# Strassen products in four PSUM banks: the second product moves from the first bank into the free half of the fourth

## The chip, the cores and the metric

The kernel runs on one core of one Trainium2 chip. The metric is device time in microseconds (us), the median of several executions; lower is better. The engines are named as in the profile: PE is TensorE (matrix products), PEld its weight loads, DVE is VectorE, ACT is ScalarE, POOL is GpSimd, SP is SyncE, which issues most of the transfers.

PSUM is the memory that TensorE writes its results to. [...] Here each accumulator is one bank, and it is used as two halves of 256 columns.

## The reference

Four graph layers run one after the other on 4096 nodes with 256 features, each as `x = layernorm(x + layer(x))`. Cut to the layers that the change touches, numbered from 0:

```python
# layer 2: one additive head
h = x @ W
e = leaky_relu((h @ a[:D])[:, None] + (h @ a[D:])[None, :], 0.01)
attention = softmax(where(adj > 0, e, -1e12), axis=1)
x = layernorm(x + elu(attention @ h))

# layer 3: cosine attention
att = softmax(where(adj > 0, cos(x @ Wk.T, x @ Wq.T), -9e15), axis=1)
x = layernorm(x + 0.5 * (att @ x) + 0.5 * x)      # every row of adj has a one
```

In both the heavy part is a product of a 4096 x 4096 matrix of weights with the 4096 x 256 features.

## The kernel before

The program is one function that works through the four layers. Layers 2 (`additive_one`) and 3 (`cosine_attention`) share the code that the change edits.

**Tiling.** The 4096 target nodes are cut into 8 blocks of 512 (index `b`). The 4096 source nodes are cut into 32 tiles of 128, taken in pairs: 16 steps `g` per block. For a pair of source tiles the weights are a tile `z` of 128 x 2 x 512 (`prob`), unnormalised; the features are two tiles of 128 x 256. What is summed over the 16 steps is the transposed output of the block, 256 features by 512 targets.

**Strassen's form.** A step is a 2 x 2 product: two source tiles, two halves of the features, two halves of the targets. Done plainly it takes eight products of 128 x 128 by 128 x 256. The kernel uses a Strassen form with seven. For this, `mix_weights` makes four combinations `s` of the weights in each step, and `mix_features` makes four combinations `t` of the features once per layer. `product` (line 440) issues product number `n` of seven; a table gives the accumulator `at`, the half, the stationary operand `w` and the moving operand `a`. An fp32 product appears in the trace as two matmul records. In layer 2, block 0 is done plainly and blocks 1 to 7 in Strassen's form; in layer 3 all eight blocks are, except for the last two steps of the last block.

**Banks before.** There are four accumulators `acc0` to `acc3`, one bank each, with one buffer each. Product 1 goes to the first half of `acc3`, products 2 and 3 to the two halves of `acc0`, products 4 and 5 to `acc1`, 6 and 7 to `acc2`. (The code counts them 0 to 6.) The second half of `acc3` is unused. The `start` flag, given with the first product that goes to a bank in step 0, begins a new sum.

**Taking the result out.** After step 15 the output quarters `c[:, 0]` to `c[:, 3]` are made by ScalarE and VectorE. `first_half` (line 449) copies product 1 out of `acc3` with ScalarE (`one`, line 451), adds it to both halves of `acc0` with one VectorE addition of 512 elements (line 452), and then adds the two halves of `acc1` one after the other (lines 454 and 455). `second_half` (line 457) adds the first half of `acc2` to two quarters (459) and its second half to one (460). As each accumulator has one buffer, the first product of the next block that writes a bank has to wait until the reads of that bank are done.

**Order of the work.** In layer 2 the order of instructions on TensorE, VectorE and ScalarE is as written out in the program (`manual_schedule`, line 649). `sums` (572) runs three steps behind `weights` (549), which makes the weights: ScalarE line 566, VectorE line 567, and the combinations with VectorE line 436 and POOL lines 437 and 438. At a block's last step `sums` comes ahead of the new block's `weights`. In layer 3 a planner in the compiler orders each engine's instructions for all but the ending; `outputs` (1184) takes a block's result out and sends its quarters through transposes (line 1151, in `squares_far`) to memory and back. `ending` (1191) does the last block, in written order again: there TensorE adds the quarters to sums that it has begun directly (line 1208). At the change from layer 2 to layer 3, the last block's quarters are projected (line 596) and finished (lines 602 to 614), while the first scores of layer 3 (line 1118) and its feature combinations (lines 429 to 432) are made.

Of the kernel before, what the change touches and what calls it, by code (L numbers as in the profile page):

```python
# [9 lines left out]
FP = mybir.dt.float32  # L10
# [4 lines left out]
OP = mybir.AluOpType  # L15
# [3 lines left out]
P = 128  # L19
# [9 lines left out]
def kernel(  # L29
# [27 lines left out]
    nc = tc.nc  # L57
# [4 lines left out]
    def pool(stack, name, bufs, **kw):  # L62
        return stack.enter_context(tc.tile_pool(name=name, bufs=bufs, reuse_waits="tile", **kw))
# [115 lines left out]
    def begin_root(mv):  # L179
        n = mv.shape[1]  # L180
        v = fin.tile([P, n], FP, name=f"v{n}")
        nc.vector.tensor_scalar_add(v, mv[:, :, 1], EPS)
        return v, first_root(v, n), n
# [240 lines left out]
    HW = QW // 2  # L424
# [15 lines left out]
    def product(acc, z, s, t, g, n):  # L440

        even, odd = X[:, 2 * g, :D], X[:, 2 * g + 1, :D]
        at, half, w, a = ((3, 0, even[:, :P], z[:, 0, :HW]), (0, 0, odd[:, :P], z[:, 1, :HW]),
                          (0, 1, t[:, 1], s[:, 2]), (1, 0, t[:, 0], s[:, 1]), (1, 1, odd[:, P:], s[:, 3]),
                          (2, 0, t[:, 2], s[:, 0]), (2, 1, t[:, 3], z[:, 1, HW:]))[n]
        nc.tensor.matmul(acc[at][:, half * HW:(half + 1) * HW], w, a, start=(g == 0 and half == 0),  # L446
                         stop=(g == NP - 1), skip_group_check=True)

    def first_half(c, one, acc):

        nc.scalar.copy(one, acc[3][:, :HW])
        nc.vector.tensor_tensor(c[:, :2, :], one.unsqueeze(1).to_broadcast([P, 2, HW]),  # L452
                                acc[0].rearrange("p (h i) -> p h i", h=2), OP.add)
        nc.vector.tensor_tensor(c[:, 2, :], c[:, 1, :], acc[1][:, :HW], OP.add)
        nc.vector.tensor_tensor(c[:, 3, :], c[:, 2, :], acc[1][:, HW:], OP.add)

    def second_half(c, acc):

        nc.vector.tensor_tensor(c[:, 1:3, :], c[:, 1:3, :], acc[2][:, :HW].unsqueeze(1).to_broadcast([P, 2, HW]), OP.add)
        nc.vector.tensor_tensor(c[:, 1, :], c[:, 1, :], acc[2][:, HW:], OP.add)  # L460

    def quarters(c, k):

        lo = k % 2 * P
        return [c[:, q, lo:lo + P] for q in ((0, 3), (1, 2))[k // 2]]
# [61 lines left out]
    def additive_one(w_sb, ga, tail, op, follow):  # L527

        with ExitStack() as lay:
# [14 lines left out]
            mixed, acc, prob, mix, mvs, roots, kept, drawn, ys, far_y = {}, {}, {}, {}, {}, {}, {}, {}, {}, {}  # L544
# [27 lines left out]
            def sums(b, g):  # L572
                if g == 0:
                    acc[b] = [pa.tile([P, QW], FP, name=f"acc{n}") for n in range(4)]
                if b:
                    for n in range(7):
                        product(acc[b], prob[b, g], mix[b, g], mixed[g // 2][:, g % 2], g, n)
                else:
                    for j in range(2 * g, 2 * g + 2):
                        for c in range(KC):  # L580
                            nc.tensor.matmul(acc[b][c], X[:, j, c * P:(c + 1) * P], prob[b, g][:, j % 2, :],
                                             start=(j == 0), stop=(j == NT - 1))
                if g == NP - 1:
                    c = kept[b] = op.tile([P, 4, HW], FP, name="quarters")
                    if b:
                        first_half(c, op.tile([P, HW], FP, name="one"), acc[b])
                        second_half(c, acc[b])
                    else:
                        nc.scalar.copy(c[:, :2, :], acc[b][0].rearrange("p (h i) -> p h i", h=2))
                        nc.vector.tensor_copy(c[:, 3, :], acc[b][1][:, :HW])  # L590
                        nc.vector.tensor_copy(c[:, 2, :], acc[b][1][:, HW:])
# [57 lines left out]
            with tc.manual_schedule(engines=fixed):  # L649
                for i in range(len(units) + LAG):  # L650
                    b, g = units[i - LAG] if i >= LAG else (-1, 0)
# [440 lines left out]
    def cosine_attention(co, tail):  # L1092
# [4 lines left out]
        with ExitStack() as lay:  # L1097
# [3 lines left out]
            cp = pool(lay, "co_parts", 1)  # L1101
# [7 lines left out]
            mixed, acc, prob, mix, y, back = {}, {}, {}, {}, {}, {}  # L1109
# [73 lines left out]

            def outputs(b):
                c = cp.tile([P, 4, HW], FP, name="quarters")
                first_half(c, cp.tile([P, HW], FP, name="one"), acc[b])
                squares_far(b, 0, (c[:, 0, :], c[:, 3, :]))
                second_half(c, acc[b])
                squares_far(b, 1, (c[:, 1, :], c[:, 2, :]))

            def ending(b):


                c = cp.tile([P, 4, HW], FP, name="quarters")
                pos = [pl.tile([P, QW], FP, name=name)[:, :D] for pl, name in ((ps, "g"), (ps, "g"), (pz, "p"), (pz, "p"))]
                rden = fin.tile([P, QB], FP, name="rden4")
                mv = [fin.tile([P, 2, 2], FP, name=f"mv_end{h}") for h in range(2)]

                def direct(k):
                    for g in range(NP - LAST, NP):  # L1200
                        for n in range(2):
                            nc.tensor.matmul(pos[k], prob[b, g][:, n, k * P:(k + 1) * P],  # L1202
                                             X[:, 2 * g + n, :D], start=(g == NP - LAST and n == 0),
                                             stop=False, skip_group_check=True)

                def others(k):
                    for n, quarter in enumerate(quarters(c, k)):
                        nc.tensor.matmul(pos[k][:, n * P:(n + 1) * P], quarter, ident, start=False, stop=True,
                                         skip_group_check=True)

                def twice_sum(k):
                    junk = cp.tile([P, D], FP, name="one")
                    nc.scalar.activation(junk, pos[k], AF.Copy, scale=2.0 / D, accum_out=rden[:, k:k + 1])

                def row(k):
                    nc.vector.reciprocal(rden[:, k:k + 1], rden[:, k:k + 1])
                    rest(b, k, pos[k], rden[:, k:k + 1], mv[k // 2][:, k % 2, :])

                def roots(h, lo, n):

                    v, r, _ = begin_root(mv[h][:, lo:lo + n])
                    return v, r, n, mv[h][:, lo:lo + n, 0]

                def lifts(v, r, n, mean):
                    end_root(v, r, n, nc.gpsimd)
                    nc.gpsimd.tensor_tensor(v, mean, r, OP.mult)
                    nc.gpsimd.tensor_scalar(v, v, -1.0, 0.0, OP.mult, OP.add)

                def scaled(k, v, r, n):
                    nc.scalar.activation(y[b][:, k, :], y[b][:, k, :], AF.Identity, bias=v[:, n:n + 1], scale=r[:, n:n + 1])  # L1230

                for k in range(2):
                    direct(k)
                first_half(c, cp.tile([P, HW], FP, name="one"), acc[b])
                second_half(c, acc[b])
                for k in range(2):
                    others(k)
                    twice_sum(k)
                    row(k)
                for k in range(2, 4):  # L1240
                    direct(k)
                    others(k)
                twice_sum(2)
                both = roots(0, 0, 2)
                row(2)
                lifts(*both)
                twice_sum(3)
                third = roots(1, 0, 1)
                scaled(0, *both[:2], 0)
                scaled(1, *both[:2], 1)  # L1250
                store(b, 0, 2, nc.sync)
                lifts(*third)
                row(3)
                v, r, _ = begin_root(mv[1][:, 1:])
                scaled(2, *third[:2], 0)
                store(b, 2, 1, nc.sync)
                s = fin.tile([P, 1], FP, name="s_end")
                nc.vector.scalar_tensor_tensor(s, r, v, r, OP.mult, OP.mult)
                nc.vector.tensor_scalar(s, s, -0.5, 1.5, OP.mult, OP.add)
                nc.vector.tensor_tensor(r, r, s, OP.mult)  # L1260
                scale_row(y[b][:, 3, :], mv[1][:, 1:], r, 0)
                store(b, 3, 1, nc.sync)
# [4 lines left out]
            for i in range(len(units) + LAG):  # L1267
                if i < len(units):
                    b, j = units[i]
# [7 lines left out]
                    if (b, j) in steps:  # L1277
                        n, step = steps[b, j]
                        co.prepare(bank, n, step, X[:, n * QB:(n + 1) * QB, :])
                if i >= LAG:  # L1280
                    b, j = units[i - LAG]
# [41 lines left out]
    with ExitStack() as weights1, ExitStack() as den1, ExitStack() as weights3:  # L1323
# [25 lines left out]
        op = weights3.enter_context(tc.tile_pool(name="gb_o", bufs=1))  # L1349
# [37 lines left out]
```

## Time and profile before

| what | value |
|---|---|
| median of 3 runs | 2798.02 us (2794.73 to 2802.38) |
| profiled execution, its own time | 2795.6 us |
| its span, from first to last instruction | 2793.8 us |
| TensorE clock granted | 1.0 |
| layer 2, blocks 1 to 7, in the span | from about 1772 us to 2165 us |
| layer 3, in the span | from about 2165 us to the end |
| copy of product 1 (line 451), ScalarE, 128 x 256 | x15, median 368 ns |
| addition of line 452, VectorE, 128 x 512 | x15, median 687 ns |
| additions of lines 454, 455, 460, VectorE, 128 x 256 | x15 each, medians 422, 417 and 419 ns |
| addition of line 459, VectorE, 128 x 512 | x15, median 681 ns |
| VectorE addition of two SBUF operands, 128 x 256 (line 437, layer 3) | x126, median 424 ns |

All times in the trace are counted from the start of the span. A line such as "1995.72 0.70 PE L446 MATMUL ... x2 [0.94 <-DVE quarters L452]" says: at 1995.72 us, for 0.70 us, TensorE ran two matmul records of line 446; before them it was idle for 0.94 us, and what released it was the VectorE instruction of line 452 that writes `quarters`. The ends of matmuls are modelled, so distances are better read from start to start. Line numbers in the quoted profile are those of the kernel before.

### The profile page before, as it was taken

How to read it: one execution, taken by the hardware profiler on the slowest of the kernel's cores; microseconds unless marked ns; L12 is line 12 of the kernel's file. 1: busy time of each engine (PE TensorE's matmuls, PEld its weight loads, DVE VectorE, ACT ScalarE, POOL GpSimd, SP SyncE). 2: the span in 40 equal slices, each digit the busy share in tenths (PEclk: the TensorE clock that was granted, in tenths of full speed). 3: DMA queues.
4: the chain of work that ended last, by engine and by line, in shares of the span. 5: the costliest groups of instructions: out<-in, count | busy, mean ns of one | idle time of the engine just before them, and what ended most of it. 6: DMA issues, size and time to landing. Idle time of an engine off the chain costs nothing. (4 is left out here: it accounts for less than half of the span.)

```text
span 2793.8 us, 50176 instructions
## 1 busy us (share of the span) xinstructions
PE 2774.1 (99%) x19445; PEld 1427.4 (51%) x19445; DVE 2289.0 (82%) x3040; ACT 1700.7 (61%) x2650; POOL 1052.5 (38%) x986
## 2 busy tenths in 40 slices
PE   9999999999999999999999999999999999999999
PEld 5333333333453333333333333788888777777776
DVE  8899999999677788887888878888887877767676
ACT  7899999999336666666666666465556422222222
POOL 0000100100029878778788793345455000000000
PEclk9999999999999999999999999999999999999999
DMA  7566676665339899998988988567778545445442
GB/s 206 107 142 137 139 144 130 137 143 114 70 97 191 186 178 196 191 188 182 197 182 189 192 181 187 168 198 207 183 207 232 121 76 82 74 71 82 75 72 44
DMA packets 275065, 411.92 MB, mean 147 GB/s; under 512 B 54809, under 2 KB 155657, under 8 KB 273930
## 3 DMA queue, kind: packets, MB, share of 16 engines
q0 software_dynamic: 104176, 182.74, 41.3%
q1 hardware_dynamic: 164280, 218.88, 26.7%
q10 hardware_dynamic: 6370, 7.10, 0.7%
q8 instruction: 152, 2.49, 0.4%
q14 instruction: 87, 0.71, 0.1%
HBM read 335.94 MB, written 39.40 MB: 134 GB/s over the span
## 5 line engine op out<-in xcount | busy, mean ns | idle before, releaser
L834 DVE TENSOR_TENSOR prob<-p,mask 128x1024 f32<-128x1024 f32 x512 | 620.0, 1222 | 166.9 <-ACT p L824 159.9
L824 ACT ACTIVATE p<-p,shift 128x1024 f32<-128x1024 f32 x512 | 557.0, 1090 | 317.8 <-PE p L822 317.1
L312 PE MATMUL acc<-prob,V 128*32 128x512 f32 x6144 | 664.0, 592 | 1.2 <-DVE prob L302 1.2
L299 ACT ACTIVATE prob<-row,dst 128x512 f32<-128x512 f32 x1020 | 635.9, 716 | 0.4
L302 DVE SCALAR_TENSOR_TENSOR prob<-prob,mask 128x2048 f32<-128x2048 f32 x256 | 580.6, 2288 | 25.8 <-ACT prob L299 24.8
L844 POOL TENSOR_TENSOR den<-den,prob 128x1024 f32<-128x1024 f32 x220 | 559.8, 2544 | 92.6 <-DVE prob L834 87.2
L822 PE MATMUL p<-qT,kT 64*64 64x512 f32 x4096 | 531.1, 590 | 2.0 <-DVE prob L834 2.0
L858 PE MATMUL acc<-prob,V 64*64 64x512 f32 x4096 | 529.9, 589 | 0.0
L312 PEld LDWEIGHTS acc<-prob,V 128*32 128x32 f32 x6144 | 197.3, 110 | 453.0 <-issue 432.2
L446 PE MATMUL acc<-mix,mixed 128*128 128x256 f32 x1428 | 388.0, 380 | 2.7 <-DVE quarters L460 1.2
L858 PEld LDWEIGHTS acc<-prob,V 64*64 64x64 f32 x4096 | 157.4, 133 | 282.1 <-issue 280.3
L822 PEld LDWEIGHTS p<-qT,kT 64*64 64x64 f32 x4096 | 154.3, 133 | 278.9 <-issue 256.5
L446 PEld LDWEIGHTS acc<-mix,mixed 128*128 128x128 f32 x1428 | 269.5, 190 | 45.0 <-PE acc L446 3.5
L90 POOL COPY tick<-prob 128x1 f32<-128x1 f32 x35 | 38.0, 1086 | 643.0 <-DVE prob L302 642.1
L1130 DVE TENSOR_TENSOR prob<-prob,mask 128x1024 f32<-128x1024 f32 x128 | 156.2, 1220 | 140.5 <-ACT prob L1122 140.1
L850 POOL DMA_DIRECT2D den<-prob x240 | 232.0, 967 | 61.0 <-DVE prob L834 22.3
L446 PE MATMUL acc<-prob,X 128*128 128x256 f32 x952 | 245.7, 380 | 3.4 <-DVE quarters L452 3.3
L1050 POOL DMA_DIRECT2D mask<-in_adjT x64 | 47.7, 745 | 530.1 <-DVE prob L1130 437.6
L446 PEld LDWEIGHTS acc<-prob,X 128*128 128x128 f32 x952 | 180.1, 190 | 84.1 <-issue 56.7
L567 DVE SCALAR_TENSOR_TENSOR prob<-r,own,mask 128x512 f32<-128x512 f32 x252 | 177.1, 744 | 51.3 <-POOL s L169 13.7
L1122 ACT ACTIVATE prob<-p 128x512 f32<-128x512 f32 x144 | 86.1, 598 | 204.1 <-PE p L1118 202.6
L1122 ACT ACTIVATE prob<-g 128x512 f32<-128x512 f32 x112 | 67.0, 598 | 208.7 <-PE g L1118 208.7
(233 smaller groups left out, 2823.1 us busy)
## 6 DMA issues: line engine op xcount, KB each, us to landing
mask<-in_adjT SPq DMA_DIRECT2D x254, 512.0 KB
den<-prob POOLq DMA_DIRECT2D x240, 512.0 KB, 5.3
mask<-edges SPq DMA_DIRECT2D x512, 64.0 KB
mask<-in_adjT POOLq DMA_DIRECT2D x64, 512.0 KB, 5.7
edges<-in_adj POOLq DMA_DIRECT2D x32, 512.0 KB, 9.6
far<-squares SPq DMA_DIRECT2D x16, 512.0 KB
den<-prob SPq DMA_DIRECT2D x16, 512.0 KB
row<-far SPq DMA_DIRECT2D x7, 1024.0 KB
```

Source lines behind the costliest of these rows:

```text
L299: nc.scalar.activation(z[:, h, :], r, AF.Relu, bias=-1.0, scale=dst[:, j, h:h + 1])
L302: nc.vector.scalar_tensor_tensor(z, z, 1.0, mask[m][:, j % MJ, :].unsqueeze(1).to_broadcast([P, H, QW]), OP.add, OP.mult)
L312: nc.tensor.matmul(acc[b][h * G:(h + 1) * G, n, :], part, prob[b, j][:, h, :], start=(j == 0), stop=(j == NT - 1))
L446: nc.tensor.matmul(acc[at][:, half * HW:(half + 1) * HW], w, a, start=(g == 0 and half == 0), stop=(g == NP - 1), skip_group_check=True)
L567: nc.vector.scalar_tensor_tensor(z[:, n, :], r, ga.own[:, j:j + 1], mask[:, n, :], OP.add, OP.mult)
L822: nc.tensor.matmul(p[c * d:(c + 1) * d, r, :], kT[half, c, at:at + d], qT[half, c, cols], start=True, stop=True)
L824: nc.scalar.activation(p, p, AF.Exp, bias=shift)
L834: nc.vector.tensor_tensor(z, p, mask[m][:, j % MJ, :].unsqueeze(1).to_broadcast([P, KC, QW]), OP.mult)
L844: nc.gpsimd.tensor_tensor(to, to, flat, OP.add)
L850: nc.gpsimd.dma_start(to, flat, accum_op=OP.add)
L858: nc.tensor.matmul(acc[b][c][r * d:(r + 1) * d, :], V[half, j, r * d:(r + 1) * d], prob[b, j][half, r, :], start=(j == 0), stop=(j == NH - 1))
L1130: nc.vector.tensor_tensor(z, z, co.mask[b, 2 * g // MJ][:, lo:lo + 2, :], OP.mult)
```

## The change

Product 2 goes to the second half of `acc3` in place of the first half of `acc0`. `acc0` then holds product 3 alone, in its second half. The start flag is given by product number (n = 0, 2, 3 and 5 begin a bank), which is again the first product of each bank.

`first_half` copies both halves of `acc3` with ScalarE: product 1 to `one`, product 2 straight to quarter 0. VectorE's first addition now makes quarter 1 alone, 256 elements. Quarter 0 still lacks product 1; an addition of 256 elements in SBUF brings it in later: at the end of `second_half` in layer 2 and in the ending, and in `outputs` of layer 3 between `first_half` and the first transposes. This adds, at each of the 15 places where a block is taken out, one ScalarE copy and one VectorE addition, and halves one VectorE addition.

```diff
         even, odd = X[:, 2 * g, :D], X[:, 2 * g + 1, :D]
-        at, half, w, a = ((3, 0, even[:, :P], z[:, 0, :HW]), (0, 0, odd[:, :P], z[:, 1, :HW]),
+        at, half, w, a = ((3, 0, even[:, :P], z[:, 0, :HW]), (3, 1, odd[:, :P], z[:, 1, :HW]),
                           (0, 1, t[:, 1], s[:, 2]), (1, 0, t[:, 0], s[:, 1]), (1, 1, odd[:, P:], s[:, 3]),
                           (2, 0, t[:, 2], s[:, 0]), (2, 1, t[:, 3], z[:, 1, HW:]))[n]
-        nc.tensor.matmul(acc[at][:, half * HW:(half + 1) * HW], w, a, start=(g == 0 and half == 0),
+        nc.tensor.matmul(acc[at][:, half * HW:(half + 1) * HW], w, a, start=(g == 0 and n in (0, 2, 3, 5)),
                          stop=(g == NP - 1), skip_group_check=True)
 
     def first_half(c, one, acc):
 
         nc.scalar.copy(one, acc[3][:, :HW])
-        nc.vector.tensor_tensor(c[:, :2, :], one.unsqueeze(1).to_broadcast([P, 2, HW]),
-                                acc[0].rearrange("p (h i) -> p h i", h=2), OP.add)
+        nc.scalar.copy(c[:, 0, :], acc[3][:, HW:])
+        nc.vector.tensor_tensor(c[:, 1, :], one, acc[0][:, HW:], OP.add)
         nc.vector.tensor_tensor(c[:, 2, :], c[:, 1, :], acc[1][:, :HW], OP.add)
         nc.vector.tensor_tensor(c[:, 3, :], c[:, 2, :], acc[1][:, HW:], OP.add)
 
-    def second_half(c, acc):
+    def second_half(c, acc, one=None):
 
         nc.vector.tensor_tensor(c[:, 1:3, :], c[:, 1:3, :], acc[2][:, :HW].unsqueeze(1).to_broadcast([P, 2, HW]), OP.add)
         nc.vector.tensor_tensor(c[:, 1, :], c[:, 1, :], acc[2][:, HW:], OP.add)
+        if one is not None:
+            nc.vector.tensor_tensor(c[:, 0, :], c[:, 0, :], one, OP.add)
...
                     if b:
-                        first_half(c, op.tile([P, HW], FP, name="one"), acc[b])
-                        second_half(c, acc[b])
+                        one = op.tile([P, HW], FP, name="one")
+                        first_half(c, one, acc[b])
+                        second_half(c, acc[b], one)
...
             def outputs(b):
                 c = cp.tile([P, 4, HW], FP, name="quarters")
-                first_half(c, cp.tile([P, HW], FP, name="one"), acc[b])
+                one = cp.tile([P, HW], FP, name="one")
+                first_half(c, one, acc[b])
+                nc.vector.tensor_tensor(c[:, 0, :], c[:, 0, :], one, OP.add)
                 squares_far(b, 0, (c[:, 0, :], c[:, 3, :]))
                 second_half(c, acc[b])
                 squares_far(b, 1, (c[:, 1, :], c[:, 2, :]))
...
                 for k in range(2):
                     direct(k)
-                first_half(c, cp.tile([P, HW], FP, name="one"), acc[b])
-                second_half(c, acc[b])
+                one = cp.tile([P, HW], FP, name="one")
+                first_half(c, one, acc[b])
+                second_half(c, acc[b], one)
```

## Prediction

> **What bounds the kernel now.** I read the page's busy times first, then the matmul groups of the changed line, then the timeline of one place where an accumulator changes hands. Two shares and the two largest groups of the products' line, from the page:
>
> ```profile
> PE 2774.1 (99%) x19445; PEld 1427.4 (51%) x19445; DVE 2289.0 (82%) x3040; ACT 1700.7 (61%) x2650; POOL 1052.5 (38%) x986
> ...
> L446 PE MATMUL acc<-mix,mixed 128*128 128x256 f32 x1428 | 388.0, 380 | 2.7 <-DVE quarters L460 1.2
> ...
> L446 PE MATMUL acc<-prob,X 128*128 128x256 f32 x952 | 245.7, 380 | 3.4 <-DVE quarters L452 3.3
> ```
>
> TensorE has work in 99% of the span, and all idle time before the products is 6.1 us, most of it released by the output additions of lines 452 and 460. So only time in which TensorE stands still can be won, and the additions are where it stands. The waits view of TensorE says the same: 3.3 us on line 452 (4 waits), 1.2 us on line 460 (6 waits).
>
> The timeline of the handover from block 4 to block 5 in layer 2 (start, duration, engine, line; idle before and its releaser in brackets), TensorE, then VectorE, then ScalarE:
>
> ```profile
> 1993.76 0.59 PE L446 MATMUL acc<-prob,mixed 128*128 128x256 f32 x2
> 1994.19 0.59 PE L446 MATMUL acc<-prob,X 128*128 128x256 f32 x2
> 1995.72 0.70 PE L446 MATMUL acc<-prob,X 128*128 128x256 f32 x2 [0.94 <-DVE quarters L452]
> 1996.26 1.14 PE L446 MATMUL acc<-mix,mixed 128*128 128x256 f32 x4
> 1997.24 0.59 PE L446 MATMUL acc<-mix,X 128*128 128x256 f32 x2
> 1998.04 0.67 PE L446 MATMUL acc<-mix,mixed 128*128 128x256 f32 x2 [0.21 <-DVE quarters L460]
> ```
> ```profile
> 1994.39 0.70 DVE L129 STREAM_TRANSPOSE squares<-rows 128x512 f32<-128x512 f32 x1
> 1995.02 0.65 DVE L452 TENSOR_TENSOR quarters<-one,acc 128x512 f32<-128x512 f32 x1
> 1995.77 0.42 DVE L454 TENSOR_TENSOR quarters<-quarters,acc 128x256 f32<-128x256 f32 x1
> 1996.23 0.42 DVE L455 TENSOR_TENSOR quarters<-quarters,acc 128x256 f32<-128x256 f32 x1
> 1996.75 0.69 DVE L459 TENSOR_TENSOR quarters<-quarters,acc 128x512 f32<-128x512 f32 x1
> 1997.47 0.42 DVE L460 TENSOR_TENSOR quarters<-quarters,acc 128x256 f32<-128x256 f32 x1
> ```
> ```profile
> 1993.63 0.38 ACT L451 COPY one<-acc 128x256 f32<-128x256 f32 x1
> 1993.88 1.52 ACT L566 ACTIVATE r<-other_row,less,dst 128x512 f32<-128x512 f32 x2
> ...
> 1998.59 1.49 ACT L566 ACTIVATE r<-other_row,less,dst 128x512 f32<-128x512 f32 x2 [2.17 <-DVE prob L567]
> ```
>
> A product is two matmul records 0.43 us together; seven make a step of 3.02 us. The first step of a new block is longer. Measured on the timeline from the first product to that of the next step: 3.57, 3.94, 4.75, 4.79, 4.36 and 4.91 us in blocks 2 to 7 of layer 2, which take over from blocks 1 to 6; together 26.3 against 6 x 3.02 = 18.1, so 8.2 us lost. Layer 3's seven handovers take 4.84 us where a usual step takes 4.74, another 0.7 us. In all 8.9 us, 0.32% of the span: the ceiling of this change.
>
> In the shown handover the second product waits for line 452 (bank 0), the fourth starts just after line 455 (bank 1; 1996.70 after 1996.65), the sixth after line 460 (bank 2; 1998.04 after 1997.89). VectorE goes through its five additions without a pause, so their chain, not TensorE, sets when the sixth product starts.
>
> [...]
>
> **The change part by part.**
>
> *Products.* Order, count and sizes stay: seven products of 0.43 us, three of the neighbouring pairs in one bank before and after. Cost 0. The program order on TensorE is the same but for one score matmul pair at the start of layer 3.
>
> *VectorE's first addition, 512 to 256 elements.* In the shown handover 452 to 454 is 0.75 us from start to start; 454 to 455, the 256 form, 0.46. So 0.29 us less, and all that follows on VectorE, through line 460, is 0.29 us earlier.
>
> *The added addition of 256 (c0 + one).* 0.42 us, some 0.34 of it new time in the queue (460 to 567 is 0.34 apart). In layer 2 it stands behind line 460, so no bank waits for it; line 567 behind it is about 0.05 us later (+0.34 - 0.29). What hides it: probabilities are made three steps ahead, and VectorE's steady share is 337 of 393 us there. Without that cover: 6 x 0.05 = 0.3 us.
>
> *ScalarE's second copy.* 0.25 to 0.37 us, and the first product of the new block now waits for both copies. In the shown handover: copies end at about 1994.02 + 0.30, first product 1994.47 instead of 1994.19, third product (the first to need bank 0) free to start at 1995.33. The 256 addition ends at 1995.02 + 0.39 = 1995.41. So ScalarE's delay is hidden, by a tenth of a microsecond only; a copy longer by that would start to show. Behind the copies on ScalarE stand line 566's activations, whose reader is line 567; ScalarE is idle 2.17 us soon after, so 0.37 us is covered. The first copy's later start costs nothing in layer 2, where ScalarE comes to it after the second product has ended.
>
> *Where the stall goes.* Second product: no wait any more. Third: starts 1995.46. Fourth: waits for line 455, now ending 1996.36, so starts 1996.41: a new stall of about 0.4 us that was hidden behind the old one. Sixth: line 460 ends 1997.60, so 1997.75 instead of 1998.04. Of the 1.1 us stall that goes, 0.8 comes back at banks 1 and 2; net 0.29. In the first handover (the 3.57 one) only the fourth and sixth waited; the sixth goes from 1827.79 to 1827.50, again 0.29. Six handovers: 6 x 0.29 = 1.7 us.
>
> *Layer 3.* Here is the VectorE order around a handover:
>
> ```profile
> 2252.89 0.69 DVE L452 TENSOR_TENSOR quarters<-one,acc 128x512 f32<-128x512 f32 x1
> 2253.61 0.45 DVE L1151 STREAM_TRANSPOSE kept<-quarters 128x256 f32<-128x256 f32 x1
> 2254.54 0.42 DVE L454 TENSOR_TENSOR quarters<-quarters,acc 128x256 f32<-128x256 f32 x1 [0.48 <-PE acc L446]
> ```
>
> The new addition stands between the first two: the transpose ends at about 2252.89 + 0.46 + 0.46 + 0.45 = 2254.26, still before 2254.54, when TensorE lets line 454 go. The 0.48 us of idle hides it, and line 460, at whose end the sixth product starts, keeps its time. The first copy starts 0.43 us later (2252.44) and ends 2252.81, before 2252.89; the second ends about 2253.15. ScalarE then waits 1.72 us for the next scores. Cost 0; without the cover, 7 x 0.2 = 1.4 us.
>
> *Layer 2 to 3.* VectorE is full from 2164.5 on and carries the extra addition with no gain (line 454 waits for TensorE there): 0.35 us later. Projections that wait for a freed bank may feel it, 0 to 0.45 us. Against it, a score pair of 0.86 us moves ahead of the projection at 2176.24, which had stalled 0.33 us. I take -0.1. *The end:* the additions end at 2780.51, their reader starts at 2781.68; the extra 0.34 is hidden.
>
> *Sum.* -1.7 - 0.1 = -1.8 us. The profiled execution took 2795.6 us with a span of 2793.8; it would take 2793.8. It lies 2.4 us below the median of the runs, 2798.0, to which I carry the difference: 2796.2.
>
> **Rivals.**
>
> (a) *The gain is taken back.* VectorE starts its chain when its own backlog lets it. If the second copy and the extra addition put that start 0.15 us later in each block, and the fourth product's new stall costs a restart of 0.11 us (the second record after a stall starts 0.32 us after the first, not 0.215), 0.29 shrinks to 0.03: 6 x 0.03 = 0.2 us, so 2797.8, or 2798.2 with a slip of 0.45 us in place of my -0.1 where layer 3 begins. Speaks for it: five of the six handovers wait behind VectorE's one queue. Against: VectorE was idle and waiting for others between blocks (line 567 for POOL, in the waits view of this stage, 37.7 us), so 0.05 us is made good there.
>
> (b) *All handover stalls vanish*: if VectorE's chain came earlier in its queue than I place it, so that banks 1 and 2 are free in time: 2798.0 - 8.9 = 2789.1. Against: line 129 stands before the first addition unchanged, and line 460 follows it by a fixed 2.5 us.
>
> (c) *Slower: ScalarE becomes late.* The first copy waits for one more product (0.43 us) and the second adds 0.37. If ScalarE had nothing to spare, each of 14 handovers would move by 0.80: +11.2, so 2809.2. It decides once ScalarE's idle time behind the copies falls under 0.8 us; the trace shows 2.17 (layer 2) and 1.72 (layer 3), and the first product already waits for line 451 in the handover at 2107.54.
>
> **How the numbers follow.** Forecast 0.55 and (a) 0.26, both within 0.3% (8.4 us, about what a measurement of this kernel can tell from no change); (b) 0.09, just beyond it; (c) 0.10, beyond it. So faster 0.09, same 0.81, slower 0.10. Effect bounds of forecast and (a): -3 (if in four handovers the whole second-product wait of 0.7 were won) to +1, so 2795 to 2799; the three runs spread over 7.7 us, half of it each way about a middle, so 2791 to 2802. (b) and (c) are mostly left out.
>
> **What would show it.** Right: no wait for line 452 before the second product; a wait of the fourth product on line 455 of 0.2 to 0.5 us; first steps near 3.3, 3.65, 4.45, 4.5, 4.1, 4.6 us; layer 3 steps still 4.84. Wrong: waits of TensorE on ScalarE's copies over 0.3 us, or steps lengthened away from the handovers.

## The result, and the profile after

The changed kernel takes 2791.9 us against 2796.1 us for the kernel before, medians of 22 runs each; the three runs of the kernel before in the table ahead, with 2798.0 as their median, are among them. The two medians lie 4.2 us apart. The ratio of the times, which is used from here on, is 0.9987, with a 95% interval of 0.9981 to 0.9993: 3.6 us less (2.0 to 5.3). The profiled execution took 2791.86 us, with a span of 2790.1.

In this section line numbers are those of the changed kernel. The first copy is line 451, the new copy 452, the first addition 453, the added addition 462 (1191 in layer 3); lines 454, 455, 459 and 460 are the same additions as before. Further down the page, 566 and 567 became 568 and 569, 504 became 506, 641 became 644, and 1151 became 1154.

The page of the changed kernel, engine shares and the two groups of products:

```profile
PE 2772.4 (99%) x19445; PEld 1427.4 (51%) x19445; DVE 2286.1 (82%) x3055; ACT 1702.6 (61%) x2665; POOL 1051.2 (38%) x986
...
L446 PE MATMUL acc<-mix,mixed 128*128 128x256 f32 x1428 | 388.6, 380 | 4.3 <-DVE mix L437 1.3
...
L446 PE MATMUL acc<-prob,X 128*128 128x256 f32 x952 | 244.3, 379 | 0.0
```

The idle time before the products that read `prob` is gone (3.4 us before). And VectorE does 15 more instructions, yet is busy 2.9 us less. Halving 15 additions and adding 15 should have cost it time: an estimate from the medians in the table ahead is 15 x (0.424 - 0.265) = 2.4 us more, with 0.265 for 0.687 - 0.422. This is the first sign that something else became shorter.

The waits view of TensorE from 1760 us on (us in total, times, longest):

```profile
PE acc L446 <- DVE mix L437: 1.3, 1, 1.3
PE acc L446 <- DVE quarters L460: 1.2, 6, 0.2
PE acc L446 <- DVE quarters L594: 1.1, 1, 1.1
PE acc L446 <- DVE quarters L455: 0.7, 3, 0.2
```

The 3.3 us on the first addition have become 0.7 us on line 455, in three handovers. The single wait of 1.3 us is in layer 3, where the kernel before had 0.4; the last section comes back to it.

The handover into block 5 again: TensorE, VectorE, ScalarE.

```profile
1991.44 1.03 PE L446 MATMUL acc<-prob,X 128*128 128x256 f32 x4
1992.36 0.67 PE L446 MATMUL acc<-mix,mixed 128*128 128x256 f32 x2
1993.25 0.70 PE L446 MATMUL acc<-mix,mixed 128*128 128x256 f32 x2 [0.22 <-DVE quarters L455]
1993.79 0.59 PE L446 MATMUL acc<-mix,X 128*128 128x256 f32 x2
1994.59 0.67 PE L446 MATMUL acc<-mix,mixed 128*128 128x256 f32 x2 [0.21 <-DVE quarters L460]
```
```profile
1991.83 0.38 DVE L453 TENSOR_TENSOR quarters<-one,acc 128x256 f32<-128x256 f32 x1
1992.32 0.42 DVE L454 TENSOR_TENSOR quarters<-quarters,acc 128x256 f32<-128x256 f32 x1
1992.78 0.42 DVE L455 TENSOR_TENSOR quarters<-quarters,acc 128x256 f32<-128x256 f32 x1
...
1994.03 0.42 DVE L460 TENSOR_TENSOR quarters<-quarters,acc 128x256 f32<-128x256 f32 x1
1994.37 0.42 DVE L462 TENSOR_TENSOR quarters<-quarters,one 128x256 f32<-128x256 f32 x1
```
```profile
1990.43 0.39 ACT L451 COPY one<-acc 128x256 f32<-128x256 f32 x1
1990.68 0.41 ACT L452 COPY quarters<-acc 128x256 f32<-128x256 f32 x1
...
1993.51 0.34 ACTq L644 DMA_DIRECT2D far_y<-y  x1
1995.48 0.78 ACT L568 ACTIVATE r<-other_row,less,dst 128x512 f32<-128x512 f32 x1 [2.00 <-DVE prob L569]
```

Products 1 and 2 run without a gap (one group of four records). Product 4 starts 0.89 us after product 3 instead of 0.43, behind line 455. Product 6 waits for line 460. From the start of the first addition to product 6 it is 2.76 us (1994.59 - 1991.83); before, it was 3.02. All this is as forecast, in this handover. What was not forecast: VectorE began its first addition 0.39 us after product 1 (1991.83 - 1991.44); before, 0.83 us after it.

Layer 3, VectorE around a handover:

```profile
2248.23 0.42 DVE L453 TENSOR_TENSOR quarters<-one,acc 128x256 f32<-128x256 f32 x1
2248.57 0.42 DVE L1191 TENSOR_TENSOR quarters<-quarters,one 128x256 f32<-128x256 f32 x1
2249.02 0.45 DVE L1154 STREAM_TRANSPOSE kept<-quarters 128x256 f32<-128x256 f32 x1
2249.88 0.42 DVE L454 TENSOR_TENSOR quarters<-quarters,acc 128x256 f32<-128x256 f32 x1 [0.41 <-PE acc L446]
```

Line 454 still waits 0.41 us for TensorE, so the added addition is covered. Layer 3's seven handover steps sum to 33.86 us in both traces.

| | before | after |
|---|---|---|
| first steps, blocks 2 to 7 of layer 2 (us) | 3.57 3.94 4.75 4.79 4.36 4.91 | 3.48 3.60 3.61 4.09 4.05 4.05 |
| their sum | 26.3 | 22.9 |
| first product of block 1 (layer 2) to first product of layer 3 | 399.25 | 395.96 |
| start of the span to block 1 of layer 2 | 1772.0 | 1770.9 |

The gain lies in layer 2, 3.3 us of it. The 1.1 us ahead of it falls in code that the change doesn't touch; over the traces of this page, in which that code is the same, the start of block 1 lies anywhere between 1769.9 and 1773.5 us. Layer 3 took 0.75 us longer in the trace after, which has the wait of 1.3 us there.

### The profile page after: what moved, and what is told of

Same layout as the page of the kernel before. It is cut to its first block, busy times and chain, and to the rows that moved or that the text cites. A ratio compares the mean times of both kernels' runs of the same rounds, so it can differ in the third digit from the quotient of the medians.

```text
span 2790.1 us, 50215 instructions
## 1 busy us (share of the span) xinstructions
PE 2772.4 (99%) x19445; PEld 1427.4 (51%) x19445; DVE 2286.1 (82%) x3055; ACT 1702.6 (61%) x2665; POOL 1051.2 (38%) x986
## 3 DMA queue, kind: packets, MB, share of 16 engines
q1 hardware_dynamic: 164280, 218.88, 26.3%
```

## Where VectorE's time went

The same stretch of VectorE's written order, in the handover from block 3 to 4: from the first addition to the second instruction `h<-X,a_row` (line 504 before, 506 after; it reads two operands from SBUF, as line 436 does). Before:

```profile
1937.98 0.65 DVE L452 TENSOR_TENSOR quarters<-one,acc 128x512 f32<-128x512 f32 x1
...
1944.86 1.05 DVE L504 CUSTOM_DVE_ANT_0 h<-X,a_row 128x256 f32<-128x256 f32 x1
...
1947.28 0.85 DVE L436 TENSOR_TENSOR mix<-prob 128x512 f32<-128x512 f32 x1
1948.05 1.72 DVE L504 CUSTOM_DVE_ANT_0 h<-X,a_row 128x256 f32<-128x256 f32 x1
```

and GpSimd beside it:

```profile
1939.06 0.59 POOL L133 DMA_DIRECT2D far<-squares  x1
1943.75 1.12 POOL L137 DMA_DIRECT2D T<-far  x2 [4.10 <-DMA far<-squares]
1944.88 0.74 POOL L437 TENSOR_TENSOR mix<-prob,mix 128x256 f32<-128x256 f32 x1
...
1948.06 0.74 POOL L438 TENSOR_TENSOR mix<-prob,mix 128x256 f32<-128x256 f32 x1
1948.75 0.73 POOL L437 TENSOR_TENSOR mix<-prob,mix 128x256 f32<-128x256 f32 x1
```

After, VectorE and GpSimd:

```profile
1935.49 0.38 DVE L453 TENSOR_TENSOR quarters<-one,acc 128x256 f32<-128x256 f32 x1
...
1941.84 1.70 DVE L436 TENSOR_TENSOR mix<-prob 128x512 f32<-128x512 f32 x1
1943.46 0.41 DVE L506 CUSTOM_DVE_ANT_0 h<-X,a_row 128x256 f32<-128x256 f32 x1
...
1945.23 1.03 DVE L436 TENSOR_TENSOR mix<-prob 128x512 f32<-128x512 f32 x1
1946.19 0.41 DVE L506 CUSTOM_DVE_ANT_0 h<-X,a_row 128x256 f32<-128x256 f32 x1
```
```profile
1936.56 0.59 POOL L133 DMA_DIRECT2D far<-squares  x1
1939.85 1.12 POOL L137 DMA_DIRECT2D T<-far  x2 [2.70 <-DMA far<-squares]
1940.98 0.74 POOL L437 TENSOR_TENSOR mix<-prob,mix 128x256 f32<-128x256 f32 x1
...
1943.68 0.78 POOL L437 TENSOR_TENSOR mix<-prob,mix 128x256 f32<-128x256 f32 x1 [0.70 <-DVE mix L436]
```

GpSimd stores the turned squares to memory (line 133) and loads them back (137). The load waits in GpSimd's own queue until the store has landed: 4.10 us before, 2.70 after. Its combinations (437, 438) stand behind that wait. Before, they came out late and back to back, on top of VectorE's instructions: line 504 took 1.05 and 1.72 us where it takes 0.41 alone. After, the backlog is shorter: over their durations alone (0.69 for line 436, 0.41 for the other) these instructions lose 1.01 and 0.34 us, both on line 436. Before, the two of line 504 lost 0.64 and 1.31, and one of line 436 lost 0.16. That is 1.35 us in place of 2.11.

Not every VectorE instruction is stretched in this way. Line 454, one of whose inputs is an accumulator in PSUM, took its usual 0.42 us beside line 438 of GpSimd, 0.39 us of it at the same time in this handover before (at 1938.73) and all of it after (at 1935.97). Lines 504 and 436, which read both inputs from SBUF, are the stretched ones here. The 1.72 us are the 0.41 of line 504 and 1.31 more, nearly twice the 0.73 of a combination; what holds the instruction up in that time is not shown.

Why did the store land earlier? ScalarE's store of the outputs, `far_y<-y`, stands on its queue behind the copies. Before, it was issued at 1939.41, 0.35 us after GpSimd's store was begun. After, the second copy puts it at 1937.17, 0.61 us after.

```profile
1939.41 0.34 ACTq L641 DMA_DIRECT2D far_y<-y  x1
```
```profile
1937.17 0.34 ACTq L644 DMA_DIRECT2D far_y<-y  x1
```

The DMA view for the stretch from 1.0 to 2.5 us after the issue of the squares' store (packets, MB, share of 16 engines; q0 carries GpSimd's transfers, q10 ScalarE's), before and then after:

```profile
q0 software_dynamic: 79, 0.32, 53.8%
q10 hardware_dynamic: 54, 0.22, 36.6%
```
```profile
q0 software_dynamic: 134, 0.52, 87.3%
q10 hardware_dynamic: 6, 0.02, 4.3%
```

Before, the two stores of 512 KB shared the engines nearly from the start. After, the squares' store went first and had nearly all of them. So a quarter of a microsecond on ScalarE decided whether it landed 4.1 to 4.8 us after its issue or 3.0 (blocks 3 to 7). By the packet times in the traces, the output store's data began to move 1.0 to 1.1 us after its issue before, and 1.8 to 1.9 us after it in the changed kernel, just when the last packet of the squares' store had begun. Why it then waited for the whole of the other store is not shown.

The theory, then: the gain is the order of two stores; it reaches TensorE through GpSimd's wait and VectorE's stretched instructions. The rivals: the bank and the shorter addition (the forecast's reason), or layer 3.

## The experiments

Times are medians. Each ratio is to runs of the kernel before on the same chip beside the experiment's own, which had medians of 2796.7 to 2798.2 us.

**The second copy alone, in the kernel before.** Banks and additions stay; in layer 2, ScalarE copies product 1 once more, to quarter 0, which the first addition then overwrites.

```diff
         nc.scalar.copy(one, acc[3][:, :HW])
+        if spare is not None:
+            nc.scalar.copy(spare, acc[3][:, :HW])
...
-                        first_half(c, op.tile([P, HW], FP, name="one"), acc[b])
+                        first_half(c, op.tile([P, HW], FP, name="one"), acc[b], c[:, 0, :])
```

> The kernel before with one more ScalarE copy of 128 x 256 behind line 451 in layer 2 alone (it writes quarter 0, which the addition of line 452 then overwrites; the result is the same). Products, banks and additions are those of before. Theory (transfer order): the copy puts ScalarE's store of the finished rows (far_y) 0.25 us later, so POOL's store of the turned squares lands about 4.1 us after the first addition instead of 5.2 to 5.9, POOL's combinations collide less with VectorE's operations of two SBUF operands, and VectorE reaches the next handover earlier: first steps of blocks 2 to 7 together about 24.6 us instead of 26.3, time about 1.7 us less. Rival (TensorE's own earlier start is what moves VectorE): landing and steps stay as before, 26.3 to 26.6 us, time 0 to +0.3 us.

Measured: 2792.4 us, ratio 0.9987 (0.9981 to 0.9994), the whole gain without the change. The first steps sum to 21.7 us. The theory had the direction right and the size small: it forecast 24.6 us, and 1.7 us off the time, which is the edge of the 3.6 measured (1.7 to 5.3). The output store is issued 1.68 us after the first addition, as in the changed kernel (1.43 before), and GpSimd's wait in the same block falls:

```profile
1935.22 0.59 POOL L133 DMA_DIRECT2D far<-squares  x1
1938.46 1.12 POOL L137 DMA_DIRECT2D T<-far  x2 [2.65 <-DMA far<-squares]
```

**The change without its second copy.** Banks and additions as changed; quarter 0 is made of twice product 1, so product 2 is left out of it.

```diff
-        nc.scalar.copy(c[:, 0, :], acc[3][:, HW:])
...
-            nc.vector.tensor_tensor(c[:, 0, :], c[:, 0, :], one, OP.add)
+            nc.vector.tensor_tensor(c[:, 0, :], one, one, OP.add)
```

> The changed kernel without the second ScalarE copy (quarter 0 is made of twice product 1 and lacks product 2; that part of the computation is left out), all additions kept. Theory (transfer order): the squares' store lands again 5.2 to 5.9 us after the first addition, and only the shorter first addition is left of the gain: first steps about 24.6 us, time 1.7 us less than before. Rival: the gain is all in the freed bank and the shorter addition, so the steps stay at 22.9 us and the time 3.5 us less than before.

Measured: 2797.0 us, ratio 1.0002 (0.9994 to 1.0011). The gain is gone, though banks and the addition of 256 are there; the 1.7 us that the theory still left to the shorter addition are not seen either (the interval runs from 1.7 us less to 3.1 more). The traced execution took 2805.2 us, 8 more than the median, so the lengths of its blocks say little. The wait of GpSimd is back:

```profile
1941.03 0.59 POOL L133 DMA_DIRECT2D far<-squares  x1
1945.84 1.12 POOL L137 DMA_DIRECT2D T<-far  x2 [4.22 <-DMA far<-squares]
```

In one block of this trace the output store happened to be issued 0.94 us behind GpSimd's, elsewhere 0.32 to 0.34; in that block, the third of the four in the table further down, VectorE's stretch C is 11.1 us, in the others 11.7 to 12.2.

**The change with an addition of 512 again.** The first addition makes quarters 1 and 2 (line 454 then overwrites the latter), which undoes only its halving.

```diff
-        nc.vector.tensor_tensor(c[:, 1, :], one, acc[0][:, HW:], OP.add)
+        nc.vector.tensor_tensor(c[:, 1:3, :], one.unsqueeze(1).to_broadcast([P, 2, HW]),
+                                acc[0][:, HW:].unsqueeze(1).to_broadcast([P, 2, HW]), OP.add)
```

> The changed kernel with its first addition widened to 512 elements again (quarters 1 and 2 both get the sum, quarter 2 is overwritten by the next addition; the result is the same). By the prediction's term of 0.29 us for each of six handovers the first steps grow from 22.9 to 24.6 us and the time is 1.7 us more than the changed kernel's, so about 1.8 us less than before. If the 256 elements are not on the path, the steps stay at 22.9 us and the time stays 3.5 us below before.

Measured: 2796.1 us, ratio 0.9995 (0.9987 to 1.0003). The interval overlaps both that of the change and no effect. The squares' store lands early here too (4.03 to 4.33 us after the first addition), so only VectorE's time is different. The first steps sum to 24.0 us, between the two forecasts, and the time, 1.3 us less than before by the ratio, lies nearer to the first. It decides nothing about the theory, and 0.29 us of VectorE's time per block may well be worth something once the store is early.

**The change in layer 3 alone, and in layer 2 alone.** The other layer keeps the old products, copies and additions.

> The change in layer 3 alone; layer 2 as before. Prediction and theory alike: VectorE's 0.48 us of idle hides it, first steps of layer 3's blocks 4.84 us as before, layer 2's first steps 26.3 us, time within 0.3 us of before. Rival (part of the gain comes from layer 3): 1 us or more less than before.

> The change in layer 2 alone: the third layer and the ending keep the old banks and the addition of 512. Every theory that has the gain in layer 2 expects nearly all of it, 3.3 to 3.6 us off the kernel before, ratio 0.9987 to 0.9988. If the third layer had a share after all, this would keep less than 2.5 us.

Measured: layer 3 alone 2797.6 us, ratio 1.0005 (0.9996 to 1.0013), with handover steps of 33.86 us; layer 2 alone 2792.9 us, ratio 0.9985 (0.9978 to 0.9991). All the gain is in layer 2.

**Only the order of the stores, in the kernel before.** The output store is issued two steps later, 6.3 us after the first addition. Nothing else is moved.

```diff
-                        nc.scalar.dma_start(far_y[b], ys[b])
+                        late.append((far_y[b], ys[b]))
...
+                        if g == 1 and late:
+                            nc.scalar.dma_start(*late.pop())
```

> The kernel before, with ScalarE's store of the finished rows (far_y, 512 KB) issued two steps later and nothing else changed: no second copy, banks and additions of before. Theory (transfer order): the squares' store lands at about 4.1 us after the first addition as with the second copy, VectorE loses about 1.2 us instead of 2 to operations stretched by POOL, and the time is 3.6 us less than before (3 to 4.7). Rival (the second copy matters for its hold on bank 3 or on ScalarE): landing or not, the time stays within 1 us of before.

Measured: 2792.1 us, ratio 0.9983 (0.9975 to 0.9990). No copy, no bank, no addition is different, and the gain is the same within the intervals.

**GpSimd's wait taken away, in the kernel before.** SP issues the loads of line 137; GpSimd's combinations no longer stand behind them. Stores as before.

```diff
-            eng.dma_start(to[q * B:(q + 1) * B], far[:, :, q, :].rearrange("a f m -> f a m"))
+            (back or eng).dma_start(to[q * B:(q + 1) * B], far[:, :, q, :].rearrange("a f m -> f a m"))
```

> The kernel before, with the four loads of the turned squares (T from far) issued from SP's queue instead of POOL's; both stores as before. Theory: the squares' store still lands late (5.2 to 5.9 us), but POOL no longer stands waiting for it with its combinations behind, so VectorE loses at most 1.2 us there and the time is 3.6 us or more less than before. Against it: SP's queue now stands about 3 us at that wait, and if mask loads come late behind it, line 567 shows waits on DMA and the gain is lost. Rival (POOL's wait has no part in it): time within 1 us of before, operations stretched as before.

Measured: 2790.5 us, ratio 0.9974 (0.9968 to 0.9981). The store landed as late as before only in block 3 (4.35 us after its issue). From block 4 on the output store came 0.45 to 0.53 us behind it, and it landed after 3.2 to 3.5 us where the trace shows it; the forecast of a late landing failed there. VectorE is equally quick in both cases (C of 9.88 us in the table further down). Four of the six first steps are down to 3.02 us, the length of any step. GpSimd goes straight from the store to its combinations, and line 504 takes its 0.41 us:

```profile
1938.15 0.58 POOL L133 DMA_DIRECT2D far<-squares  x1
1942.14 0.72 POOL L437 TENSOR_TENSOR mix<-prob,mix 128x256 f32<-128x256 f32 x1 [3.41 <-DVE mix L436]
```
```profile
1944.15 0.41 DVE L504 CUSTOM_DVE_ANT_0 h<-X,a_row 128x256 f32<-128x256 f32 x1
...
1946.54 0.42 DVE L504 CUSTOM_DVE_ANT_0 h<-X,a_row 128x256 f32<-128x256 f32 x1
```

**Both moves together.**

> Both moves on the kernel before: the rows' store two steps later and the squares' loads from SP. If the theory holds and SP's masks are not late: at least the better of the two alone, 4 to 6 us less than before, with first steps of blocks 2 to 7 under 21 us together (18.1 would be no stall at all). If masks come late: no better than the late store alone.

Measured: 2790.9 us, ratio 0.9978 (0.9969 to 0.9986), no different from the loads on SP alone; the first steps sum to 19.2 us. The two moves act on one wait.

**The change, with the loads on SP.** The same edit as above, on the changed kernel.

> The change, with the loads of the squares' transposes issued by SP instead of GpSimd. Theory (the change works only through the moment at which GpSimd gets past its wait for the squares' store): with that wait off GpSimd the change has nothing left to shorten, so this takes what the kernel before takes with the loads on SP, 2790.5, within 0.1% (2788 to 2793, ratio 0.9965 to 0.9985). Rival (the bank change has a gain of its own, in the handovers): 3.6 us less than that, 2787.

Measured: 2790.1 us, ratio 0.9972 (0.9965 to 0.9980), against 0.9974 (0.9968 to 0.9981) for the kernel before with the same edit. Where GpSimd doesn't wait, the change is worth nothing that can be measured. Both are faster than the kernel before; against the change alone (0.9981 to 0.9993) their intervals lie lower, and just touch it in one of the two.

**The change, with the output store two steps later.**

> The change, with the store of the outputs issued two steps later, as it was done to the kernel before. Theory (the change's gain is that this store no longer runs ahead of the squares' store): the squares' store already lands some 4.05 us after the first addition, so moving the other one further away brings nothing more, 2792, ratio 0.998 to 0.999. Rival (the two gains are separate and add up): 3.6 plus 5.2 us, 2788, ratio 0.997.

Measured: 2795.2 us, ratio 0.9990 (0.9981 to 0.9998). That is 3 us above the 2792 of the theory, but the kernel before was slower on this chip too (2798.2), and the ratio is at the upper end of the forecast. The rival's sum of both gains, 0.997, is excluded. Whether the edit costs something of its own can't be told: the interval holds the 0.9987 of the change, and the profiled execution had a wait of 4.0 us in layer 3 (the last section). Its first steps sum to 21.0 us, less than the change's 22.9, and yet its layer 2 was 396.8 us long, 0.8 more: block 1 alone took 1.2 us longer, with 2.3 us of VectorE's waits for masks from memory where the changed kernel had 0.4.

**More work for VectorE, in the kernel before.** One addition of 256 in SBUF behind line 460, in layer 2.

```diff
                         second_half(c, acc[b])
+                        nc.vector.tensor_tensor(one, one, one, OP.add)
```

> The kernel before with one more VectorE addition of 256 SBUF elements behind line 460 in layer 2 (it doubles a tile that is no longer read; the result is the same). The prediction's term for the added addition, hidden behind line 460: 0 us, at most 0.3. Theory now (VectorE with ScalarE and POOL is a loop that sets layer 2's pace from block 2 on, so its work counts wherever it stands): 6 x 0.34 = 2.0 us more than before.

Measured: 2797.8 us, ratio 1.0003 (0.9994 to 1.0011): inconclusive, 1.7 us less to 3.1 us more. Its trace doesn't decide it either, as the next part shows.

**What sets the length of a block.** Let C be VectorE's time from the start of a handover's first addition to the end of the second `h<-X,a_row`, and P the time from one first addition to the next. Both are read from the VectorE timeline for four successive handovers, the second to the fifth (the differences are taken before rounding):

| kernel | C (us) | P (us) | P - C |
|---|---|---|---|
| before | 11.76 11.80 11.35 12.04 | 57.01 57.04 56.62 57.30 | 45.25 45.25 45.26 45.26 |
| after | 10.63 11.11 11.09 11.06 | 55.87 56.34 56.31 56.30 | 45.24 45.23 45.21 45.24 |
| before, second copy | 10.59 10.56 10.56 10.57 | 55.83 55.81 56.26 55.81 | 45.25 45.25 45.70 45.24 |
| after, no second copy | 11.65 11.91 11.09 12.19 | 56.90 59.07 56.79 57.44 | 45.25 47.16 45.70 45.25 |
| change in layer 3 alone (layer 2 as before) | 11.95 11.93 12.18 12.19 | 57.19 57.17 57.42 57.41 | 45.24 45.25 45.25 45.21 |
| before, store later | 10.57 11.46 11.05 11.05 | 55.80 56.69 56.28 56.27 | 45.23 45.22 45.23 45.22 |
| before, one more addition | 11.61 12.53 12.10 12.19 | 56.84 57.78 57.33 57.41 | 45.23 45.25 45.24 45.23 |
| before, loads on SP | 9.88 9.88 9.88 9.88 | 55.10 55.21 55.28 55.27 | 45.22 45.33 45.40 45.38 |
| after, loads on SP | 9.95 9.94 9.96 9.95 | 55.35 55.16 55.18 55.16 | 45.40 45.22 45.23 45.22 |

Outside C a round of VectorE's work takes 45.2 to 45.3 us, so what is won or lost inside C moves the next handover by just as much. The exceptions without the loads on SP, 47.16 and twice 45.70, are just the rounds in which VectorE waited for a mask from memory, 0.5 to 1.2 us. The rounds of VectorE, ScalarE and GpSimd, which wait for one another, are longer than TensorE's block, which is some 55.2 us where nothing holds it up (P with the loads on SP); TensorE catches up with them at each handover and stands still there for the difference. Only with the loads on SP is C short enough for TensorE to be the slower one: P - C then grows beyond 45.26 in some rounds, and first steps are 3.02 us. The change takes 0.77 us off C (11.74 to 10.97) and 0.79 us off P; over the four rounds that is 3.15 us, nearly all of the 3.3 in layer 2.

C varies between traces of the same layer 2: it is 11.7 us on average in the kernel before, and 12.1 with the change in layer 3 alone. So the 12.1 of the last experiment can't be put down to its added addition, and its first steps, 27.5 us in place of 26.3, can't either. What the change's own additions do to C is seen where GpSimd stretches nothing: with the loads on SP it is 9.88 us without the change and 9.95 with it.

## Why the prediction was right and wrong

**Right in place and size of the single steps.** The second product's wait on line 452 is gone. In the shown handover the fourth product has the forecast stall of 0.4 us behind line 455 (0.46 measured). The first addition to the sixth product takes 0.26 us less, forecast 0.29. The first copy does follow product 2 now: in layer 3's handover it starts 1.07 us after product 1 of the last step (2247.73 after 2246.66), behind a wait of 0.27 us for TensorE; before, 0.69 us after it (2252.01 after 2251.32), without a wait. ScalarE's copies cost TensorE nothing, with 2.00 us of idle time left behind them where 2.17 were. Layer 3 is worth nothing that can be measured, by its steps and by the run with layer 3 alone. The direction was right, and 2791.9 lies inside the range, at its lower end. The mechanism is not what put it there: the range of the effect itself, -3 to +1 us, ends short of -3.6, and it was the 3.9 us added for the spread of the runs that took 2791.9 in. (With these 3.9 us its upper end comes out at 2803, not at 2802.)

**Wrong in the sum.** The forecast was 1.8 us less; it is 3.6 (2.0 to 5.3). The step that failed is "Six handovers: 6 x 0.29 = 1.7 us". It took the start of VectorE's chain as given, and counted what the chain lost after it. But that start is where VectorE's own round has brought it. The change makes the additions inside C 0.29 us shorter and adds one of 0.34, so by itself it leaves the round as long as it was: 0.05 us more. With the loads on SP this is measured: 9.88 us became 9.95. The run without the second copy agrees: a ratio of 1.0002, with C at 11.7 us on average as before. The prediction had these 0.05 us, and held them to be covered; VectorE's order has no such cover, since P follows C. The 0.29 us was real within the handover and still no gain, since the following handover began as late as ever. Of the six first steps that the prediction listed, three came within 0.2 us (3.48 for 3.3, 3.60 for 3.65, 4.05 for 4.1); the others were 0.4 to 0.8 us shorter than forecast. No run isolates its -0.1 us at the change of layers.

**What was left out.** On ScalarE the prediction went from the second copy to the activations of line 566 and their cover of 2.17 us, and stopped. It did not name the output store (line 641) that is queued behind the copies, nor the transfer of GpSimd that this store runs beside. To be late by 0.25 us was counted as a cost that is hidden; it was the gain. None of the views that the prediction rests on shows it: GpSimd's wait is not among TensorE's waits, and a stretched VectorE instruction counts as busy, not as waiting.

**The rivals.** (a) had the right mechanism, a VectorE that starts its chain when its own backlog lets it, with the wrong sign: it saw only the added work. The argument against it, that VectorE's idle time between blocks makes a delay good, failed: P grows with C by the same amount in the table. (b) named the condition that was met in part, "if VectorE's chain came earlier in its queue than I place it": against product 1, it came 0.9, 0.4, 0.05 and 0.6 us earlier in blocks 4 to 7 of layer 2. The argument against it, that line 460 follows line 129 by a fixed 2.5 us, is true and beside the point. With the loads on SP, (b) nearly came about: handover steps of 19.6 us, of an ideal 18.1. (c) did not come: no wait on a copy appears in the waits view of the changed kernel. With the loads on SP one does, of 0.3 us on the second copy.

**What stays open.** Whether the halved addition is worth something once the stores are in the new order: 0.9995 (0.9987 to 1.0003) with 512 elements and 0.9987 (0.9981 to 0.9993) with 256 overlap. What makes one store wait for the whole of another, in place of sharing the engines with it, is open too.

## What to carry to other kernels

When an engine feeds the busy one in rounds, measure the length of its round between two of the same instructions, and ask what in it a change makes shorter; here a stall at a handover was the difference of two rounds, and 0.29 us off the handover's additions alone left it there (ratio 1.0002 without the second copy). Follow a delayed engine's queue past its arithmetic to the transfers that it issues, and from each to the transfers beside it and to the engine that waits for their landing. And try a load that waits for a store's landing on another queue than that of an engine that has arithmetic to do behind it; here that edit alone gave a ratio of 0.9974.

## What the runs showed of the hardware

- An instruction lengthened fourfold without any wait in the trace: line 504, 0.41 us alone, took 1.72 beside two GpSimd combinations of 0.73; line 436, 0.69 alone, took 1.70. The groups view shows it as a mean of 767 ns (before) against 501 (after) and 481 (loads on SP) for 24 instructions of the same form.
- Two stores of 512 KB, on two queues, issued 0.35 us apart, shared the engines; issued 0.61 us apart, they went one after the other. The first of them landed 4.1 to 4.8 us after its issue in the former case, 3.0 in the latter. With the loads on SP, a distance of 0.33 us gave 4.35, and one of 0.45 gave 3.5.
- In layer 3 one wait differs from execution to execution: the products wait for line 437 of VectorE, for 0.4 us in the trace before, 1.3 after, and 4.0 to 4.3 us in four of the experiments. In the trace of the change with the later store, VectorE stood 8.1 us ahead of it, for a transfer:

```profile
2509.32 0.69 DVE L1171 TENSOR_REDUCE rden<-kept 128x2 f32<-128x512 f32 x1 [8.10 <-DMA kept<-away]
```

TensorE's granted clock was then 0.80 and 0.78 on average over two stretches of 4 us (2508 to 2516), with 1.00 in the stretch before them and in the two after. In the trace with the change in layer 3 alone, whose wait was 4.0 us too, it was 0.50 and 0.66 (2512 to 2520). After the 1.3 us wait of the changed kernel it stayed at 1.00 (2504 to 2524). What lowers it, and after how long a wait, is not shown. The transfer belongs to code that no experiment changed. From the first product of layer 3 to the end of the span, the four traces with the long wait take 627.4 to 628.4 us, all others 622.3 to 624.3; the four executions lie 3.2 to 8.2 us above the medians of their kernels. So this wait makes part of the spread between runs of one kernel; why the transfer is late in some of them was not tested.
